# Mamba and mixture-of-experts layer: identity transposes in PE's first gaps, and due times of its own for the second sequence

## The chip, the core and the metric

The kernel runs on one core of a Trainium2 chip. Its engines are TensorE (PE, with its weight loads shown as PEld), VectorE (DVE), ScalarE (ACT), GpSimd (POOL) and SyncE (SP, which only issues transfers here). The metric is the time of one execution on the device, in microseconds (us); lower is better.

## What is computed

The input is 16 sequences of 256 positions with 256 features, all float32. Each sequence is normalised, then goes through two independent layers, and the sum of both and of the input is the output.

```python
xn = _layernorm(x, axis=-1)
x = x + _L0_attn_ref(xn, ...) + _L0_ffn_ref(xn, ...)

# _L0_attn_ref: a state-space (Mamba) layer, 512 channels, 16 states each
proj = jnp.einsum('blh,he->bel', input_states, W_in)
hidden, gate = jnp.split(proj, 2, axis=1)
x = lax.conv_general_dilated(hidden, conv_kernel, ...)[..., :l]      # 4 taps for each channel
hidden = jax.nn.silu(x + conv_bias[None, :, None])
dt, Bm, Cm = jnp.split(ssm_p, [TR, TR + N], axis=-1)                 # ssm_p = hidden x W_x
dts = jax.nn.softplus(jnp.einsum('blr,re->ble', dt, W_dt) + b_dt)
dA = jnp.exp(dts[..., None] * A[None, None])
dBu = dts[..., None] * Bm[:, :, None, :] * hs_ble[..., None]
state = a * state + bu                                               # scan over the positions
y = jnp.einsum('ben,bn->be', state.astype(dtype), c)
y = (scan_out + hidden * D[None, :, None]) * jax.nn.silu(gate)
return jnp.einsum('bel,eh->blh', y, W_out)

# _L0_ffn_ref: 32 experts of width 96, the 8 best of each position, weighted by softmax
rw, sel = jax.lax.top_k(probs, K)
h = jax.nn.silu(x @ wg) * (x @ wu)
acc + h @ wd * w_e[:, None]
```

## The kernel before

All 32 experts are computed densely for every position, and the routing weight (zero for the experts not chosen) scales the hidden values. So for each sequence PE does the same list of products: the turned input (`turn`, L379), the router (`route`, L394), two projections (`project`, `ph`, L517), the step parameters (`params`, `px`, L555, and `widen`, L578), the gate (`pgate`, L697), the output (`po`, L723), and for the experts 24 times a gate product (`pg`), an up product (`pu`, both L471) and a down product (`acc`, L506).

The other engines stand between these. For the Mamba side ACT begins the convolution (L529), DVE adds its other taps (L540), and ACT applies silu (`activate`, `hs`, L547). POOL forms the scan's input (`feed`, `bu`, L630), ACT the decays (`decay`, `da`, L644), DVE runs the scans (L652) and multiplies by C (`read`, `pr`, L664), and an accumulating transfer that POOL issues adds the states up in `y` (L669). For the experts ACT takes the silu of two gate products at once (`silu`, `sg`, L484), POOL multiplies it by the routing weights (`weigh`, L490), which SP has spread over the partitions from memory (`spread`, L457), and DVE multiplies by the up product (`combine`, `h`, L494).

The tiles live in rings of buffers. In PSUM these are g (2 banks), u (2 banks), acc (1 buffer) and da (3 buffers). The gate products and `px` take banks of ring g, the up products banks of ring u.

The order of the work is not written by hand. A planner (class `Plan`, in Python, at build time) holds each step with an engine, a length in us, what it needs, which ring buffers it takes and gives back, and a due time. It plays the program forward, and whenever an engine is free it takes, among the steps that are ready and whose buffers are free, the one with the smallest due time. The order so found is the program; on the chip the waits follow from it, and each engine works in its order. The functions on ACT need tables. A step that names another table than the loaded one costs a table load, and a step whose table is loaded, or that needs none, has `STAY` taken off its due time.

The due time of a step of sequence b is a base time plus offsets by kind:

```python
t = ORIGIN + PERIOD * b
e = ORIGIN + RATE * b + LEAD
due += DUE.get(kind, 0.0) + (FIRST.get(kind, 0.0) if b == 0 else 0.0)
due += LAST.get(kind, 0.0) if b == B - 1 else 0.0
```

The base is `t` for the Mamba side and `e` for the experts. `DUE` holds the offsets of all sequences, `FIRST` and `LAST` are added for the first and for the last one. `EARLY` gives for some kinds how long before its due time a step may start.

At the start PE does 14 transposes of the identity (`warm`, L335 to L338) in a bank of ring g, before any input has come. Then come the router's weights, turned (`turn_router`, L326), and the first x (`turn` of sequence 0). The planner holds `warm` with 6.0 us.

Of the kernel before, what the change touches and what calls it, by code (L numbers as in the profile page):

```python
# [19 lines left out]
class Plan:  # L20
# [7 lines left out]
    SWITCH = 1.3  # L28
    HANDOVER = dict(PE=0.27, DVE=0.14, ACT=0.12, POOL=0.1, SP=0.1)
    MARGIN = dict(PE=0.4, DVE=0.1, ACT=0.1, POOL=0.1, SP=0.0)  # L30
    STAY = 8.6

    def __init__(self, rings):
        self.size = rings
# [86 lines left out]
def mamba_moe_kernel(  # L121
# [30 lines left out]
    nc = tc.nc  # L152
    P = 128
    B, L, H = x.shape
# [7 lines left out]
    SPS = L // P  # L162
# [15 lines left out]
    SLOWEST = 1e-26  # L178
    ORIGIN = -8.4
    PERIOD = 79.3  # L180
    RATE = 79.8

    DUE = dict(
        load_x=-120.5, stats=-16.5, root=-64.0, invert=-262.0, norm=218.5, turn=-490.0,
        keep_turned=-136.0, route=-110.0, largest=-337.5, expo=50.5, choose=-1121.5,
        send_weights=-122.5, project=-72.0, conv_first=402.5, conv_rest=236.0, activate=-361.5,
        params=-140.5, keep_params=-203.5, send_params=-258.5, widen=-105.5, steps=-57.0,
        skip=99.0, inputs=-255.0, fetch=-414.5, feed=399.0, decay=-22.0, scan=427.0, read=68.9,
        collect=-162.5, spread=41.0, gates=-37.5, ups=607.5, silu=230.0, weigh=115.0,
        combine=-69.0, down=114.0, settle=-364.0, gate=38.0, gate_silu=-13.0, fold=508.5,  # L190
        gated=598.5, project_out=-129.5, load_again=-28.5, finish=5.5,
    )
    EARLY = dict(
        load_x=169.0, load_experts=25.0, stats=37.0, turn=155.0, route=255.0, project=501.0,
    )

    FIRST = dict(
        route=248.0, largest=4.5, expo=0.5, choose=551.5, project=287.5, conv_first=-504.5,
        conv_rest=-239.5, activate=150.0, params=-457.5, keep_params=163.5, widen=6.0, steps=770.5,
        skip=-277.5, inputs=137.5, fetch=-152.0, feed=-250.0, decay=-61.0, scan=-50.5, read=-70.5,  # L200
        collect=-120.5, spread=-96.0, gates=-48.0, ups=-216.5, silu=-173.5, weigh=271.5,
        combine=239.0, down=-66.5,
    )

    LAST = dict(
        fetch=-293.5, feed=1.0, decay=252.5, scan=589.0, read=109.5, collect=-95.0, spread=0.5,
        gates=198.5, ups=131.0, silu=192.0, weigh=-110.0, combine=538.5, down=189.5, settle=2.5,
        gate=7.5, gate_silu=223.0, fold=-22.5, gated=238.5, project_out=-415.5, finish=519.5,
    )
    LEAD = -29.6  # L210
    TOPK = 8
    EPS = 1e-5

# [6 lines left out]
    ps = ctx.enter_context(tc.tile_pool(name="ps", bufs=1, space=PSUM))  # L220
# [8 lines left out]
    def take(pool, ring, shape, nm):  # L229
        i = taken[ring] % RINGS[ring]  # L230
        taken[ring] += 1
        return pool.tile(shape, F32, tag=f"{ring}_{i}", name=nm)
# [3 lines left out]
    live = {}  # L236
# [66 lines left out]
    ident = const.tile([P, P], F32, name="ident")  # L303
# [16 lines left out]
    def bank(nm, kind):  # L320
        return take(ps, kind, [P, 512], nm)
# [11 lines left out]


    def warm():  # L335
        pr = bank("warm", "g")
        for i in range(14):
            nc.tensor.transpose(pr[:, :P], ident, ident)  # L338


    def stats(b):
# [405 lines left out]
    b = 0  # L747
# [3 lines left out]
    def add(kind, key, engine, length, due, *args, early=None, **kw):  # L751
        fn = kw.pop("fn", None) or steps_of[kind]
        if early is None:
            early = EARLY.get(kind, 1e9)
        due += DUE.get(kind, 0.0) + (FIRST.get(kind, 0.0) if b == 0 else 0.0)
        due += LAST.get(kind, 0.0) if b == B - 1 else 0.0
        plan.add((kind, *key), engine, length, due, fn, *args, early=early, **kw)

    steps_of = dict(
        load_x=load_x, stats=stats, root=root, invert=invert, norm=norm, turn=turn,  # L760
        keep_turned=keep_turned, route=route, largest=largest, expo=expo, choose=choose,
        project=project, conv_first=conv_first, conv_rest=conv_rest, activate=activate,
        params=params, keep_params=keep_params, widen=widen, steps=steps, skip=skip, inputs=inputs,
        fetch=fetch, spread=spread, gates=gates, ups=expand, silu=silu, combine=combine,
        weigh=weigh, down=down, settle=settle, gate=gate, gate_silu=gate_silu, gated=gated,
        project_out=project_out, load_again=load_again, finish=finish, store=store, feed=feed,
        add_skip=add_skip, fold=fold, send_params=send_params, send_weights=send_weights, collect=collect, decay=decay, scan=scan, read=read,
        turn_router=turn_router, keep_router=keep_router, warm=warm, grow=grow, shrink=shrink, load_router=load_router, load_in=load_in,
        load_steps=load_steps, load_out=load_out, load_experts=load_experts,
    )  # L770
    add("load_router", (), "SP", 0.5, -200.0, lands=3.0)
    add("warm", (), "PE", 6.0, -500.0, takes=[("g", "warm")], gives=["warm"])
    add("turn_router", (), "PE", 0.8, -90.0, needs=[("load_router",)], takes=[("g", "prw")])
    add("keep_router", (), "ACT", 0.3, -89.0, needs=[("turn_router",)], gives=["prw"])
    add("load_in", (0,), "SP", 512 * KB, -199.0, 0, lands=2.0)
# [3 lines left out]
    for j in range(PARTS):  # L779
        for i, kind in enumerate("gud"):  # L780
            due = ORIGIN + LEAD + RATE / PARTS * j + 4.0 * i
# [3 lines left out]
    for b in range(B):  # L785
# [4 lines left out]
            needs=[("turn", b - 1)] if b else [], lands=11.0 if b else 3.5)  # L790
        add("stats", (b,), "DVE", 0.9, t, b, needs=[("load_x", b)],
            takes=[("mv", ("mv", b)), ("st", ("st", b)), ("std", ("rs", b))], gives=[("st", b)])
# [3 lines left out]
            gives=[("mv", b)])  # L796
        add("norm", (b,), "ACT", 1.09, t, b, needs=[("invert", b)],
            gives=[("rs", b)])
        xT = ("xnT", b)
        add("turn", (b,), "PE", 1.0, t, b, needs=[("norm", b)], gives=[x],  # L800
            takes=[("u", ("pt", b)), ("xnT", xT)])
        add("keep_turned", (b,), "ACT", 0.6, t, b, needs=[("turn", b)],
            gives=[("pt", b)])
        add("route", (b,), "PE", 0.9, t if b else t + 30.0, b, needs=[("keep_turned", b), ("keep_router",)],
            takes=[("g", ("pl", b)), ("nmax", ("nmax", b)), ("rest", ("rest", b))], gives=[xT])
# [7 lines left out]
        for q in range(2):  # L813
            add("project", (b, q), "PE", 4 * MM, t, b, q, needs=[("keep_turned", b)] + last + ([("project", b, 0)] if q else []),
                takes=[("gu"[q], ("ph", b, q))] + ([] if q else [("hs", hs)]), gives=[xT])
            add("conv_first", (b, q), "ACT", 0.92, t, b, q, gives=[("ph", b, q)],
                needs=[("project", b, q)] + ([("conv_first", b, 0)] if q else []))
            add("conv_rest", (b, q), "DVE", 2.4, t, b, q,
                needs=[("conv_first", b, q)], gives=[("ph", b, q)])
        add("activate", (b,), "ACT", 1.1, t, b, table="silu",  # L820
            needs=[("conv_rest", b, q) for q in range(2)])
        add("params", (b,), "PE", 8 * MM, t, b, needs=[("activate", b)] + ([] if b else [("load_steps",)]),
            takes=[("g", ("px", b)), ("dt", ("dt", b))])
        add("keep_params", (b,), "ACT", 0.63, t, b, needs=[("params", b)], gives=[("px", b)])
        add("send_params", (b,), "SP", 0.5, t, b, needs=[("keep_params", b)], lands=6.5)
        for q in range(2):
            add("widen", (b, q), "PE", 2 * MM, t, b, q,
                needs=[("keep_params", b)] + ([("widen", b, 0)] if q else []),
                takes=[("gu"[q], ("pdt", b, q))] + ([] if q else [("dts", dts)]),
                gives=[("dt", b)])  # L830
            add("steps", (b, q), "ACT", 0.86, t, b, q, gives=[("pdt", b, q)], table="softplus",
                needs=[("widen", b, q)] + ([("steps", b, 0)] if q else []))
        for c in range(EC):
            u, j = divmod(c, CPU)
            add("skip", (b, c), "ACT", 0.42, t, b, c,
                needs=[("activate", b)] + ([("skip", b, c - 1)] if c else []),
                takes=[] if c else [("sk", ("sk", b))], gives=[hs])
        add("inputs", (b,), "POOL", 2.5, t, b, needs=[("steps", b, 0), ("steps", b, 1),
            ("params", b)] + [("skip", b, c) for c in range(EC)])
        for g in range(GROUPS):  # L840
            at = t + PERIOD / GROUPS * g
            add("fetch", (b, g), "SP", 512 * KB, at, b, g, needs=[("send_params", b)],
                takes=[("rep", ("rep", b, g))], lands=5.5, early=14.0)

        for r in range(UNITS):
            k = UNITS * b + r
            g, u = divmod(r, PAIRED)
            at = t + PERIOD / UNITS * r
            add("feed", (k,), "POOL", 2.31, at, k, needs=[("fetch", b, g), ("inputs", b)],
                takes=[("bu", ("bu", k))], gives=[hs])  # L850
            for j in range(CPU):
# [3 lines left out]
                    takes=[("da", ("da", m))], gives=[dts], table="exp")  # L855
                add("scan", (m,), "DVE", 1.12, when, m, needs=[("decay", m), ("feed", k)],
                    gives=[("bu", k)])
                add("read", (m,), "DVE", 0.6, when, m,
                    needs=[("scan", m)] + ([("read", m - 1)] if j else []),
                    takes=[] if j else [("pr", ("pr", k)) if g else (f"y{u}", ("y", b, u))],  # L860
                    gives=[("da", m), ("rep", b, g)])
            reads = [("read", CPU * k + j) for j in range(CPU)]
            if b == B - 1 and g == GROUPS - 1:
                add("collect", (k,), "DVE", 1.25, at + PERIOD / SLOTS, k, fn=collect_last,
                    needs=reads + [("fold", b, u)], gives=[("pr", k)])
                continue
            if g == 0:
                add("collect", (k,), "POOL", 0.61, at + PERIOD / SLOTS, b, u, fn=add_skip,
                    needs=reads, gives=[("sk", b)], lands=6.5)
                continue  # L870
            add("collect", (k,), "POOL", 0.61, at + PERIOD / SLOTS, k,
                needs=reads + [("collect", k - PAIRED)],
                gives=[("pr", k)], lands=7.8)

        e = ORIGIN + RATE * b + LEAD
        for i in range(PARTS):
            add("spread", (b, i), "SP", 3.0, e + RATE / PARTS * i, b, i,
                needs=[("send_weights", b)], takes=[("wr", ("wr", b, i))], lands=6.0, early=20.0)
        for i in range(PAIRS // BATCH):
            at = e + RATE * BATCH / PAIRS * i  # L880
            qs = range(BATCH * i, BATCH * (i + 1))
            for q in qs:
                part = 2 * q // CPG
                add("ups", (b, q), "PE", 4 * MM, at, b, q, "u", gives=[xT], takes=[("u", ("u", b, q))],
                    needs=[("keep_turned", b)] + ([] if b else [("load_experts", part, "u")]))
                add("weigh", (b, q), "POOL", 1.23, at, b, q, gives=[("wr", b, part)],
                    needs=[("silu", b, i), ("spread", b, part)])
                add("combine", (b, q), "DVE", 0.6, at, b, q,
                    needs=[("weigh", b, q), ("ups", b, q)],
                    takes=[("h", ("h", b, q))], gives=[("u", b, q), ("sg", b, q)])  # L890
                add("down", (b, q), "PE", 4 * MM, at, b, q, gives=[("h", b, q)],
                    needs=[("combine", b, q)] + ([("down", b, q - 1)] if q else [])
                    + ([] if b else [("load_experts", part, "d")]),
                    takes=[] if q else [("acc", ("acc", b))])
            add("gates", (b, i), "PE", 8 * MM, at, b, i, gives=[xT],
                needs=[("keep_turned", b)] + ([] if b else [("load_experts", part, "g")]),
                takes=[("g", ("g", b, q)) for q in qs])
            add("silu", (b, i), "ACT", 1.09, at, b, i, needs=[("gates", b, i)],
                takes=[("sg", ("sg", b, q)) for q in qs], gives=[("g", b, q) for q in qs],
# [3 lines left out]
            gives=[("acc", b)])  # L903

        add("gate", (b,), "PE", 8 * MM, t, b, gives=[xT],
            takes=[(r, (r, "gate", b, q)) for q in range(2) for r in ("g", "gs")],
            needs=[("keep_turned", b)] + ([] if b else [("load_in", 1)]), early=10.0)
        add("gate_silu", (b,), "ACT", 1.09, t, b, needs=[("gate", b)],
            gives=[("g", "gate", b, q) for q in range(2)], table="silu")
# [51 lines left out]
```

## Time and profile before

| what | us |
|---|---|
| median of the runs (lowest to highest, 3 runs) | 1326.89 (1322.99 to 1330.68) |
| the profiled execution, its own time | 1322.61 |
| its span, from the first to the last instruction | 1320.8 |
| mean granted TensorE clock over the span | 0.996 |
| ACT busy in scan decays (`da`, L644) | 468.9 |
| DVE busy in scans (`da`, L652) | 608.2 |
| POOL busy in scan inputs (`bu`, L630) | 715.5 |
| idle time of PE ahead of `pu`, put down to `h` of DVE | 8.6 |

The profile is of one execution. Busy times are those of an engine's instructions. Matmuls overlap, so a busy PE need not be at its peak, and a matmul at half clock counts as busy too. Idle time of an engine is shown ahead of the instruction that ended it, with the instruction that released it behind an arrow. All times on a timeline are counted from the span's start.

### The profile page before, as it was taken

To read this page: it belongs to the slowest core of one execution; us is meant where nothing else is said; L and a number is where in the kernel's file an instruction comes from. 1 tells how busy PE (TensorE), PEld (TensorE's weight loads), DVE (VectorE), ACT (ScalarE), POOL (GpSimd) and SP (SyncE) were. 2 spreads that over 40 slices of the span, in tenths; PEclk is the share of its full clock that TensorE was granted. 3 is DMA by queue.
4 is the path that set the end of the run, shared out by engine and by line. 5 is a ranking of instruction groups with operands and counts; after the bars stand their busy time and mean duration, and the time that the engine had idled before them with its cause. 6 is when DMAs were issued, how large, how long until landed. Compare 5 with 4: busy or idle time off the path is not lost.

```text
span 1320.8 us, 18891 instructions
## 1 busy us (share of the span) xinstructions
PE 1290.6 (98%) x5968; PEld 1108.5 (84%) x5968; DVE 1178.9 (89%) x1735; ACT 1129.6 (86%) x1895; POOL 1184.6 (90%) x803
## 2 busy tenths in 40 slices
PE   8999999999999999999999999999999999999998
PEld 6878888878888887888888888888888888888887
DVE  3688999899989999989999898998989899899986
ACT  5888798888888988899898998989899898988873
POOL 0789899989998998998999999998999989898995
PEclk9999999999999999999999999999999999999999
DMA  9998898898988999999899998999889899998994
GB/s 252 238 254 190 193 212 208 198 210 192 216 187 178 217 219 203 199 197 216 189 216 199 219 204 185 217 198 216 199 194 216 191 205 198 208 205 192 196 222 93
DMA packets 174035, 268.79 MB, mean 204 GB/s; under 512 B 37840, under 2 KB 112112, under 8 KB 173936
## 3 DMA queue, kind: packets, MB, share of 16 engines
q0 software_dynamic: 40672, 124.80, 50.4%
q1 hardware_dynamic: 130624, 142.75, 39.9%
q8 instruction: 47, 0.77, 0.2%
q10 hardware_dynamic: 2640, 0.05, 0.1%
q14 instruction: 52, 0.43, 0.1%
HBM read 137.51 MB, written 5.24 MB: 108 GB/s over the span
## 4 chain that ended last, share of the span: by engine, by line
PE 56%; DVE 13%; POOL 10%; DMA 8%; issue 7%; ACT 5%; SPq 0%; ACTq 0%; POOLq 0%; DVEq 0%
PE pu L471 14%; PE acc L506 14%; PE pg L471 13%; DVE da L652 6%; DMA rep<-bcd 5%; POOL bu L630 4%; PE px L555 4%; DVE pr L664 3%; PE po L723 3%; POOL sg L490 3%; PE ph L517 3%; PE pgate L697 2%; ACT da L644 2%; POOL y L669 2%; PE pdt L578 2%
## 5 line engine op out<-in xcount | busy, mean ns | idle before, releaser
L630 POOL TENSOR_TENSOR bu<-rep,hs 128x1024 f32<-128x1024 f32 x256 | 715.5, 2947 | 68.2 <-DVE da L652 44.2
L652 DVE TENSOR_TENSOR_SCAN da<-da,bu 128x512 f32<-128x512 f32 x512 | 608.2, 1216 | 40.1 <-ACT da L644 36.2
L644 ACT ACTIVATE da<-dts,a_sb 128x256 f32<-128x256 f32 x1024 | 468.9, 473 | 88.2 <-DVE pr L664 64.7
L471 PE MATMUL pu<-xnT,wu_sb 128*128 128x256 f32 x1536 | 361.7, 381 | 9.5 <-DVE h L494 8.6
L506 PE MATMUL acc<-wd_sb,h 128*128 128x256 f32 x1536 | 363.2, 379 | 0.9 <-DVE h L494 0.8
L471 PE MATMUL pg<-xnT,wg_sb 128*128 128x256 f32 x1536 | 349.9, 381 | 4.0 <-ACT sg L484 3.2
L490 POOL TENSOR_TENSOR sg<-sg,wr 128x512 f32<-128x512 f32 x192 | 318.2, 1971 | 34.8 <-ACT sg L484 34.4
L471 PEld LDWEIGHTS pu<-xnT,wu_sb 128*128 128x128 f32 x1536 | 291.3, 191 | 52.3 <-DVE h L494 11.7
L471 PEld LDWEIGHTS pg<-xnT,wg_sb 128*128 128x128 f32 x1536 | 292.4, 191 | 47.0 <-ACT sg L484 5.3
L669 POOL DMA_DIRECT2D y<-pr x222 | 319.8, 1446 | 9.7 <-DVE pr L664 3.7
L506 PEld LDWEIGHTS acc<-wd_sb,h 128*128 128x128 f32 x1536 | 291.2, 190 | 41.3 <-DVE h L494 2.0
L664 DVE TENSOR_TENSOR pr<-da,rep 128x512 f32<-128x512 f32 x448 | 294.2, 677 | 3.4 <-DMA y<-pr 1.6
L644 ACT ACT_TABLE_LOAD x148 | 189.9, 1283 | 2.6
L494 DVE TENSOR_TENSOR h<-pu,sg 128x512 f32<-128x512 f32 x192 | 131.1, 683 | 52.0 <-POOL sg L490 25.3
L484 ACT ACTIVATE sg<-pg 128x512 f32<-128x512 f32 x192 | 105.3, 594 | 8.3 <-PE pg L471 5.5
L484 ACT ACT_TABLE_LOAD x81 | 103.9, 1283 | 3.0 <-PE pg L471 1.6
L540 DVE SCALAR_TENSOR_TENSOR hs<-ph,small,hs 128x255 f32<-128x255 f32 (+2 forms) x192 | 76.1, 471 | 0.0
L713 POOL TENSOR_TENSOR y<-y,gs 128x512 f32<-128x512 f32 x30 | 74.3, 2953 | 0.1
L555 PE MATMUL px<-hs,wx_sb 128*32 128x256 f32 (+1 forms) x256 | 62.8, 393 | 3.0 <-ACT sg L484 3.0
L723 PE MATMUL po<-wout_sb,y 128*128 128x256 f32 x256 | 60.9, 381 | 4.1 <-POOL y L713 3.1
L517 PE MATMUL ph<-xnT,win_sb 128*128 128x256 f32 x256 | 64.3, 397 | 0.0
L688 POOL TENSOR_TENSOR y<-y 128x512 f32<-128x512 f32 x32 | 63.9, 2399 | 0.1
(65 smaller groups left out, 868.5 us busy)
## 6 DMA issues: line engine op xcount, KB each, us to landing
y<-pr POOLq DMA_DIRECT2D x222, 512.0 KB, 7.4
rep<-bcd SPq DMA_DIRECT2D x128, 512.0 KB, 6.1
wr<-wd SPq DMA_DIRECT2D x128, 192.0 KB, 5.4
wr<-wd SPq DMA_DIRECT2D x128, 128.0 KB, 5.5
wr<-wd SPq DMA_DIRECT2D x128, 64.0 KB, 5.3
y<-sk POOLq DMA_DIRECT2D x32, 256.0 KB, 5.9
xt<-L_attn_input_states_dram SPq DMA_DIRECT2D x16, 256.0 KB, 5.7
o<-L_attn_input_states_dram SPq DMA_DIRECT2D x16, 256.0 KB, 6.8
```

Source lines behind the costliest of these rows:

```text
L471: nc.tensor.matmul(p[:, j, :], w[:, hc, ts(c, P)], xs[:, hc, :], start=(hc == 0), stop=(hc == HC - 1),)
L484: nc.scalar.activation(sg, live.pop(("g", b, q)), AF.Silu)
L490: nc.gpsimd.tensor_mul(sg, sg, wr[:, r : r + 2, :])
L494: nc.vector.tensor_mul(h, live.pop(("u", b, q)), live.pop(("sg", b, q)))
L506: nc.tensor.matmul(acc[:, s, :], h[:, j, ts(s, P)], wd_sb[:, c, :], start=(c == 0 and s == 0), stop=(c == FC - 1), skip_group_check=True,)
L517: nc.tensor.matmul(ph[:, j, :], win_sb[:, hc, ts(2 * q + j, P)], xs[:, hc, :], start=(hc == 0), stop=(hc == HC - 1),)
L555: nc.tensor.matmul(p, w[:, c, :], hs[:, c, :], start=(c == 0), stop=(c == EC - 1))
L630: nc.gpsimd.tensor_mul(bu, live["rep", b, g][:, 0:1].to_broadcast([P, CPU, NG, L]), live["hs", b][:, ts(u, CPU), :].unsqueeze(2).to_broadc ...
L644: nc.scalar.activation(da[:, i, :], dts[:, c, :], AF.Exp, scale=a_sb[:, c, n : n + 1])
L652: nc.vector.tensor_tensor_scan(flat, flat, live["bu", k][:, j].rearrange("p n l -> p (n l)"), 0.0, op0=ALU.mult, op1=ALU.add,)
L664: nc.vector.tensor_mul(live["pr", k][:, j], live.pop(("da", m)), live["rep", b, g][:, 1])
L669: nc.gpsimd.dma_start(live["y", b, u].rearrange("p c n l -> p (c n l)"), live.pop(("pr", k)).rearrange("p c n l -> p (c n l)"), accum_op=A ...
```

## The change

`warm` takes its tile from ring acc in place of ring g, and no longer gives it back. A new step `keep_warm` does more transposes of the identity in the same tile: six when the router's weights have been turned, four when the first x has been turned; the second gives the buffer back. The planner's length of `warm` goes from 6.0 to 4.6. A new dict `SECOND` is added to the due times of sequence 1. All other dicts and the constants `STAY`, `RATE` and `LEAD` have new values; `PERIOD` and `ORIGIN` stay. No step of the computation itself is added, removed or cut in another way.

```diff
-    STAY = 8.6
+    STAY = 18.7
...
-    RATE = 79.8
+    RATE = 79.2
...
     DUE = dict(
...
-        load_x=-120.5, stats=-16.5, root=-64.0, invert=-262.0, norm=218.5, turn=-490.0,
+        load_x=-227.0, stats=-16.5, root=60.0, invert=-103.5, norm=315.5, turn=-525.0,
...
-        collect=-162.5, spread=41.0, gates=-37.5, ups=607.5, silu=230.0, weigh=115.0,
+        collect=-168.5, spread=70.0, gates=-34.5, ups=744.0, silu=177.0, weigh=182.5,
...
     EARLY = dict(
-        load_x=169.0, load_experts=25.0, stats=37.0, turn=155.0, route=255.0, project=501.0,
+        load_x=163.0, load_experts=1.0, stats=37.0, turn=13.0, route=225.0, project=631.0,
     )
...
     FIRST = dict(
...
-        collect=-120.5, spread=-96.0, gates=-48.0, ups=-216.5, silu=-173.5, weigh=271.5,
+        read=98.0, collect=-165.0, spread=-304.5, gates=-69.5, ups=-284.5, silu=-159.0,
...
+    SECOND = dict(
+        load_x=-154.5, stats=-69.0, root=-107.0, invert=-72.5, norm=250.5, turn=38.5,
+        keep_turned=-111.0, route=96.0, largest=-100.5, expo=-59.0, choose=13.0,
+        send_weights=-47.5, project=53.0, conv_first=45.5, conv_rest=-55.0, activate=-26.0,
+        params=1.5, keep_params=0.5, send_params=39.5, widen=69.0, steps=36.5, skip=203.5,
+        inputs=-47.0, fetch=-97.5, feed=47.0, decay=-75.5, scan=89.5, read=40.0, collect=-93.5,
+        spread=4.5, gates=-3.5, ups=-204.5, silu=85.5, weigh=-61.0, combine=24.0, down=147.0,
+        settle=-68.5, gate=5.5, gate_silu=-12.5, fold=123.0, gated=-9.5, project_out=-29.5,
+        load_again=-7.0, finish=-55.5,
+    )
...
-    LEAD = -29.6
+    LEAD = -28.8
...
     def warm():
-        pr = bank("warm", "g")
-        for i in range(14):
-            nc.tensor.transpose(pr[:, :P], ident, ident)
+        live["warm"] = take(ps, "acc", [P, SPS, H], "warm")
+        keep_warm(14)
+
+
+    def keep_warm(count):
+        for i in range(count):
+            nc.tensor.transpose(live["warm"][:, 0, :P], ident, ident)
...
         due += DUE.get(kind, 0.0) + (FIRST.get(kind, 0.0) if b == 0 else 0.0)
+        due += SECOND.get(kind, 0.0) if b == 1 else 0.0
...
-    add("warm", (), "PE", 6.0, -500.0, takes=[("g", "warm")], gives=["warm"])
+    add("warm", (), "PE", 4.6, -500.0, takes=[("acc", "warm")])
+    add("keep_warm", (1,), "PE", 1.3, -490.0, 6, needs=[("turn_router",)])
+    add("keep_warm", (2,), "PE", 0.8, -490.0, 4, needs=[("turn", 0)], gives=["warm"])
```

More of the change, by code (lines that the diff above doesn't have):

```diff
@@ L180, in mamba_moe_kernel @@
     PERIOD = 79.3
-    RATE = 79.8
+    RATE = 79.2
     DUE = dict(
-        load_x=-120.5, stats=-16.5, root=-64.0, invert=-262.0, norm=218.5, turn=-490.0,
[L185 to L188, printed above, removed]
-        collect=-162.5, spread=41.0, gates=-37.5, ups=607.5, silu=230.0, weigh=115.0,
-        combine=-69.0, down=114.0, settle=-364.0, gate=38.0, gate_silu=-13.0, fold=508.5,
-        gated=598.5, project_out=-129.5, load_again=-28.5, finish=5.5,
+        load_x=-227.0, stats=-16.5, root=60.0, invert=-103.5, norm=315.5, turn=-525.0,
+        keep_turned=-191.5, route=-108.0, largest=-330.5, expo=181.0, choose=-1176.5,
+        send_weights=-270.5, project=-11.0, conv_first=565.0, conv_rest=249.0, activate=-364.0,
+        params=-161.0, keep_params=-256.5, send_params=-231.5, widen=-198.5, steps=-84.5,
+        skip=155.0, inputs=-291.5, fetch=-267.5, feed=336.0, decay=-39.0, scan=499.0, read=54.9,
+        collect=-168.5, spread=70.0, gates=-34.5, ups=744.0, silu=177.0, weigh=182.5,
+        combine=-139.0, down=231.0, settle=-483.5, gate=33.0, gate_silu=21.5, fold=501.0,
+        gated=721.0, project_out=-35.0, load_again=-24.0, finish=41.5,
@@ L192, in mamba_moe_kernel @@
     )
     EARLY = dict(
-        load_x=169.0, load_experts=25.0, stats=37.0, turn=155.0, route=255.0, project=501.0,
+        load_x=163.0, load_experts=1.0, stats=37.0, turn=13.0, route=225.0, project=631.0,
     )
     FIRST = dict(
-        route=248.0, largest=4.5, expo=0.5, choose=551.5, project=287.5, conv_first=-504.5,
-        conv_rest=-239.5, activate=150.0, params=-457.5, keep_params=163.5, widen=6.0, steps=770.5,
-        skip=-277.5, inputs=137.5, fetch=-152.0, feed=-250.0, decay=-61.0, scan=-50.5, read=-70.5,
@@ L201, in mamba_moe_kernel @@
-        collect=-120.5, spread=-96.0, gates=-48.0, ups=-216.5, silu=-173.5, weigh=271.5,
-        combine=239.0, down=-66.5,
+        route=226.0, largest=50.5, expo=-140.0, choose=605.0, project=291.0, conv_first=-613.0,
+        conv_rest=-473.0, activate=178.5, params=-415.0, keep_params=180.0, widen=-45.5,
+        steps=918.5, skip=-362.5, inputs=212.0, fetch=-196.0, feed=-325.5, decay=-113.5, scan=-2.5,
+        read=98.0, collect=-165.0, spread=-304.5, gates=-69.5, ups=-284.5, silu=-159.0,
@@ new lines, in mamba_moe_kernel @@
+        weigh=204.0, combine=285.0, down=32.0,
+    )
[8 more added lines that the diff above has]
+        load_again=-7.0, finish=-55.5,
@@ L203, in mamba_moe_kernel @@
     )
     LAST = dict(
-        fetch=-293.5, feed=1.0, decay=252.5, scan=589.0, read=109.5, collect=-95.0, spread=0.5,
-        gates=198.5, ups=131.0, silu=192.0, weigh=-110.0, combine=538.5, down=189.5, settle=2.5,
-        gate=7.5, gate_silu=223.0, fold=-22.5, gated=238.5, project_out=-415.5, finish=519.5,
+        fetch=-110.5, feed=8.5, decay=300.5, scan=555.0, read=-52.0, collect=-306.5, spread=-123.0,
+        gates=198.5, ups=84.0, silu=464.5, weigh=-183.0, combine=520.0, down=355.0, settle=-92.0,
@@ L209, in mamba_moe_kernel @@
+        gate=-58.0, gate_silu=123.0, fold=-114.5, gated=367.0, project_out=-485.5, finish=535.0,
     )
-    LEAD = -29.6
+    LEAD = -28.8
     TOPK = 8
@@ L767, in mamba_moe_kernel @@
         add_skip=add_skip, fold=fold, send_params=send_params, send_weights=send_weights, collect=collect, decay=decay, scan=scan, read=read,
-        turn_router=turn_router, keep_router=keep_router, warm=warm, grow=grow, shrink=shrink, load_router=load_router, load_in=load_in,
+        turn_router=turn_router, keep_router=keep_router, warm=warm, keep_warm=keep_warm, grow=grow, shrink=shrink, load_router=load_router, load_in=load_in,
         load_steps=load_steps, load_out=load_out, load_experts=load_experts,
```

## The prediction

> **What bounds the kernel now.** I read the page's busy shares first. Five engines are all above 85%, and a 98% for PE says little, because it is a mean over stages.
>
> ```profile
> PE 1290.6 (98%) x5968; PEld 1108.5 (84%) x5968; DVE 1178.9 (89%) x1735; ACT 1129.6 (86%) x1895; POOL 1184.6 (90%) x803
> ```
>
> So I cut the span into stages and asked for the busy time of each engine in each (columns: stage, its length, busy time of PE, PEld, DVE, ACT, POOL with counts, granted TensorE clock, DMA share, GB/s).
>
> ```profile
> 8.47:31.78 23.31, 20.30 (x73) 15.75 (x74) 9.52 (x33) 12.81 (x21) 2.50 (x2) 0.93 0.96 281
> 31.78:78.00 46.22, 45.60 (x217) 38.84 (x216) 31.72 (x54) 39.69 (x65) 35.13 (x23) 1.00 0.93 242
> 78.00:120.00 42.00, 37.40 (x156) 31.37 (x155) 37.10 (x50) 34.41 (x60) 36.29 (x24) 0.92 0.97 222
> 120.00:660.00 540.00, 527.85 (x2455) 452.13 (x2454) 500.95 (x730) 469.45 (x797) 502.58 (x337) 1.00 0.90 202
> 660.00:1160.00 500.00, 499.97 (x2345) 433.94 (x2344) 460.13 (x680) 451.03 (x751) 467.04 (x317) 1.00 0.93 205
> 1160.00:1316.90 156.90, 154.48 (x712) 132.65 (x710) 137.50 (x185) 118.75 (x200) 140.29 (x96) 1.00 0.84 183
> ```
>
> Length minus PE busy is PE's idle time: 3.01, 0.62, 4.60, 12.15, 0.03 and 2.42 us. From 660 to 1160 PE never stops: the matrix products are the bound, and no new order can gain there. After 1316.9 only a sum and the store remain (3.9 us). What can be won lies in the idle time, and in stretches where PE runs slowly while it counts as busy. For these I read PE's own timeline at the start (start, length, instruction, count, idle time before it).
>
> ```profile
> 1.37 3.25 PE L338 MATMUL warm<-ident 128*128 128x128 f32 x14 [1.37 <-POOL eps_sb L306]
> 4.55 0.42 PE L326 MATMUL prw<-ident,rw_sb 32*128 32x32 f32 x2
> 6.40 1.40 PE L379 MATMUL pt<-ident,xt 128*128 128x128 f32 x4 [1.44 <-ACT xt L370]
> 8.47 1.91 PE L394 MATMUL pl<-rwT,xnT 128*128 128x32 f32 x8 [0.68 <-ACT xnT L384]
> 10.20 6.44 PE L517 MATMUL ph<-xnT,win_sb 128*128 128x256 f32 x16
> 16.47 3.62 PE L471 MATMUL pg<-xnT,wg_sb 128*128 128x256 f32 x16
> 19.93 3.62 PE L471 MATMUL pu<-xnT,wu_sb 128*128 128x256 f32 x16
> 26.55 5.23 PE L555 MATMUL px<-hs,wx_sb 128*32 128x256 f32 x16 [3.01 <-ACT sg L484]
> ```
>
> Two groups stand out. The 16 products `ph` take 6.44 us, and the 16 of the same shape right after them 3.62. The 16 `px` take 5.23 us, but 3.77 in the chain that ended last at 234.03. Both are half-clock work. For `px` the clock column says so (0.50 from 26 to 29). For `ph` it shows 1.00; there the durations are the evidence, the column is not. ACT's timeline tells why PE was idle ahead of `px`:
>
> ```profile
> 21.53 1.06 ACT L547 ACTIVATE hs<-hs 128x1024 f32<-128x1024 f32 x1
> 22.60 1.28 ACT L353 ACT_TABLE_LOAD   x1
> 23.90 0.30 ACT L353 ACTIVATE rstd<-mv,eps_sb 128x2 f32<-128x2 f32 x1
> ...
> 24.61 1.28 ACT L484 ACT_TABLE_LOAD   x1
> 25.90 1.09 ACT L484 ACTIVATE sg<-pg 128x512 f32<-128x512 f32 x2
> ```
>
> Between two uses of the silu table ACT goes to sqrt and back for the root of the second sequence. `px` needs a bank of ring g, and both hold `pg` until `sg` has read them.
>
> **The change, part by part.** The sum is made against the profiled execution: 1322.61 us, span 1320.8. It is at the fast end of the runs shown; the median 1326.89 lies 4.28 above it, which I add at the end.
>
> *The identity in the gaps.* Six transposes go behind the router's, four behind the first x. At the 231 ns between such transposes in the `warm` row they need 1.39 and 0.92 us; the idle times there are 1.44 and 0.68. The first six fit. The four would delay the router's products by 0.24 us if the clock is still low, and fit at 141 ns each (the weight load of later transposes): 0 to +0.25, I take 0. The `warm` tile moves from ring g to ring acc, whose first product starts at 35.51, so nobody waits for it.
>
> *What an open clock gives.* `ph` 6.44 - 3.62 = 2.8 us; the router's 8 products at 231 - 141 ns for each load, 0.7. Together 3.5, all of it on PE's path. In the trace the first burst is busy from 1.37 to 4.97 = 3.6 us, and yet the work behind it stayed slow up to about 15.8. The Trainium skill ("TensorE: Matmul & The Clock Gate", Part 1: The HAM clock gate) says that one busy window of about 3.4 us opens the clock, that the windows run free of the kernel's start, and that the ramp is best not fitted. By that rule 3.6 us of transposes can be enough already, the addition gains nothing in such a run, and my sum is smaller by 3.5. By the row they were not enough: a window must fall wholly inside, and only a longer burst ensures that. With the gaps filled, PE is busy from 1.37 to 8.5, which holds a whole window wherever it begins. Bounds 0 (a transposed identity doesn't count, or this run's window was unlucky in before and others were not) to 3.5; I take the row, 3.5.
>
> *The order on ACT.* A step's due time is its stage's plus the dicts' offsets, less STAY if its table is loaded. Before, when `activate` of sequence 0 ends: silu(0,0) is -38.0 + 230 - 173.5 = 18.5, less 8.6 = 9.9; root(1) is 70.9 - 64 = 6.9. Root wins. After: silu(0,0) is -37.2 + 177 - 159 - 18.7 = -37.9; root(1) is 70.9 + 60 - 107 = 23.9. Silu wins by far. So `sg` follows `hs` directly, 25.90 - 22.60 = 3.3 us sooner, one table load (1.28) is saved, and PE's 3.01 us wait goes. With it the clock doesn't drop, and `px` needs 3.77 instead of 5.23: 1.46 more. 4.47 together. What is late next: `hs` itself, behind DVE's convolution. That starts at 15.30, after `ph`; with faster `ph` it is held by the routing steps on DVE (11.27 to 13.18, 0.7 earlier), so it starts near 12.5, and `hs` and `sg` end near 19.8 and 20.9. PE gets to `px` at 23.55 - 3.5 = 20.0: 0.9 of wait is left. Net of both: -3.5 - 4.5 + 0.9 = -7.1 us.
>
> Does it pass on? The first `h` waits for POOL, and POOL needs the weights' rows, which SP starts to spread at 19.66 behind the routing. This moves by 0.7 at most. In after, `px` ends at 20.9 + 3.8 = 24.7, one more batch of `pg` fills PE to 28.2, and the first `h` is there at 28.6 even unmoved. So 0.4 is lost: -6.7.
>
> *Due times of the second sequence.* Two waits carry this stage, with the slow clock behind them:
>
> ```profile
> 97.74 3.63 PE L471 MATMUL pu<-xnT,wu_sb 128*128 128x256 f32 x8 [2.54 <-DVE h L494]
> ...
> 113.61 5.41 PE L471 MATMUL pg<-xnT,wg_sb 128*128 128x256 f32 x16 [1.89 <-ACT sg L484]
> ```
>
> Idle 4.4; slow work 3.63 - 1.89 (8 products elsewhere) and 5.41 - 3.62, 3.5: 7.9 in all. The new offsets act on just these steps, but which wait goes can't be read from a trace of before. Bounds: -7.9, and +2.5 (one more wait like the longer). I take half the gain, -4.0: the two waits have different causes, and one removed brings its clock with it.
>
> *STAY, RATE and the other offsets.* A longer STAY saves table loads (308 at 1283 ns, 395 us of ACT). The dense stage hides them all: there they are worth 0. In 120:660 and the last stage the 14.6 us of idle may go or grow. From -14.6 to +20 (below); I take 0, as no row favours a side.
>
> Sum: -6.7 - 4.0 = -10.7; 1322.61 - 10.7 = 1311.9; plus 4.28, 1316.2: **1316 us**, 0.8% faster. About 0.5% (1320.3 to 1333.5) is what a measurement of this kernel can tell from no change.
>
> **Rivals.** *The later stalls go too:* the other half of the second sequence and half of 14.6: -11.3 more, 1305. For it: the idle of 120:660 is a handful of waits (2.54 for POOL's `y` at 228, 2.24 for `h` at 282), not steady. Against: DVE and POOL are 93% busy there, with little room to catch up.
>
> *The clock isn't opened:* identity transposes may not count, and the first 3.25 us of them opened nothing. Then 3.5 is missing: 1319.5.
>
> *The head start is swallowed:* the scan work on DVE and POOL (93%) sets when PE gets its `y` and `h`, and what PE gains early it waits for before 660. About 3 us survive: 1324, no change. For it: 12.15 us of PE idle follow the ramp now.
>
> *Slower: STAY turns into a wait in every sequence.* ACT holds exp up to 18.7 us past a silu's due time; ring g has two banks, one batch of `pg` fills both, and PE, in order, stops behind it. Now this wait costs PE 3.2 us in all. If it comes once a sequence, at the 2.4 us of the stalls seen, in 14 sequences: 33.6 - 14.6 there now = +19, with the -10.7: 1335. It decides from (14.6 + 10.7) / 14 = 1.8 us a sequence. Against it: in the dense stage PE has about 0.03 us of idle, so buffers now cover the switches; ACT is 90% busy there.
>
> **How the numbers follow.** Forecast 0.34, later stalls too 0.20, clock not opened 0.12, swallowed 0.18, slower 0.16. Faster by over 0.5%: the first two and two thirds of the third, 0.62; within: 0.22; slower: 0.16. The range goes from 1303, just under the better case, to 1332, which cuts most of the slower one.
>
> **What would show it.** Right: `ph` x16 in about 3.6 us; `sg` right behind `hs` on ACT with no sqrt load between; `px` in 3.8 us, ending near 25; less than 1.2 us of PE idle before it; 78:120 with under 3 us of PE idle and a clock above 0.95. Wrong: `ph` still over 6 us; a `pg` or `pu` wait of 2 us that returns every 79 us beyond 660; or the head 7 us early and 120:660 with some 20 us of idle.

## The result: slower by 0.9%, and the profile after

The changed kernel takes 1337.47 us (median of 6 runs, 1331.53 to 1340.64) beside 1324.76 for the kernel before. The ratio is 1.009, with a 95% interval from 1.0068 to 1.0113. The profiled execution has a span of 1336.0 us, 15.2 more than before. Lines moved by 11 to 15: `nmr`, L361 before, is L376 now, `h` L509, `bu` L645.

First the busy shares on the page, then the same stages as in the prediction (length, busy time of PE, PEld, DVE, ACT, POOL with counts, granted clock, DMA share, GB/s).

```profile
PE 1295.0 (97%) x5978; PEld 1111.4 (83%) x5978; DVE 1185.3 (89%) x1735; ACT 1132.6 (85%) x1897; POOL 1184.1 (89%) x803
```

```profile
8.47:31.78 23.31, 23.16 (x101) 19.14 (x100) 9.42 (x33) 15.44 (x28) 4.33 (x4) 1.00 0.95 268
31.78:78.00 46.22, 45.16 (x211) 38.12 (x209) 33.99 (x57) 40.06 (x67) 31.69 (x20) 1.00 1.00 246
78.00:120.00 42.00, 33.83 (x145) 28.48 (x146) 35.91 (x47) 32.11 (x52) 38.47 (x26) 0.96 0.91 206
120.00:660.00 540.00, 517.20 (x2382) 441.33 (x2380) 491.97 (x718) 460.23 (x777) 490.66 (x332) 0.99 0.90 197
660.00:1160.00 500.00, 498.69 (x2332) 432.19 (x2333) 459.68 (x674) 449.56 (x748) 465.21 (x314) 1.00 0.93 204
```

PE's idle time is 0.15, 1.06, 8.17, 22.80 and 1.31 us; before it was 3.01, 0.62, 4.60, 12.15 and 0.03. The first stage lost its wait, as forecast. The two behind it gave 4.0 us back, and 120 to 660 lost another 10.7. The busy shares on the page hardly show this: PE goes from 98 to 97%, the others move by at most a point.

What PE waits for shows it better (in all, times, longest). First a row of before, then the same row of the changed kernel:

```profile
PE acc L506 <- DVE h L494: 0.8, 1, 0.8
```

```profile
PE acc L521 <- DVE h L509: 20.8, 14, 4.1
```

In the new order the experts' down product comes to PE before its `h` is there, 14 times in place of once.

The head, on PE's timeline and on ACT's:

```profile
10.26 5.53 PE L532 MATMUL ph<-xnT,win_sb 128*128 128x256 f32 x16
...
22.84 3.84 PE L570 MATMUL px<-hs,wx_sb 128*32 128x256 f32 x16
```

```profile
21.24 1.06 ACT L562 ACTIVATE hs<-hs 128x1024 f32<-128x1024 f32 x1
22.20 1.06 ACT L499 ACTIVATE sg<-pg 128x512 f32<-128x512 f32 x2
```

`sg` follows `hs` with no table load between, `px` starts without a wait and at full clock, and it ends at 26.68 in place of 31.78: 5.1 us ahead. `ph` still takes 5.53 us, so in this execution PE came to full clock only inside it.

Where do the 22.8 us come from? The first long stall of PE is `acc` at 191.38, which waits 4.12 us for `h`. In DVE's queue this `h` stands behind one small instruction (the products `pr` between them are left out):

```profile
185.27 4.26 DVE L376 SCALAR_TENSOR_TENSOR nmr<-mv,rstd 128x2 f32<-128x2 f32 x1
...
190.65 0.67 DVE L509 TENSOR_TENSOR h<-pu,sg 128x512 f32<-128x512 f32 x1
```

What `nmr` waits for is seen most clearly at 361: two of DVE's lines, then two of POOL's for the same time.

```profile
360.54 0.15 DVE L373 RECIPROCAL rstd<-rstd 128x2 f32<-128x2 f32 x1
360.72 4.31 DVE L376 SCALAR_TENSOR_TENSOR nmr<-mv,rstd 128x2 f32<-128x2 f32 x1
```

```profile
360.70 3.09 POOL L645 TENSOR_TENSOR bu<-rep,hs 128x1024 f32<-128x1024 f32 x1
363.01 2.00 POOL L505 TENSOR_TENSOR sg<-sg,wr 128x512 f32<-128x512 f32 x1
```

`nmr` works on two elements a partition and takes 0.16 us when POOL has no product under way. Here it takes 4.31 and ends at 365.03, when POOL's second product ends (363.01 + 2.00 = 365.01). (POOL's records overlap a little, and its spans are rough.) In the traces of both kernels each `nmr` of over 1 us, 20 in all, ends 15 to 29 ns after the end of a product of POOL, and up to three such products end while it waits. DVE works in order, so what stands behind `nmr` waits as well: at 185 the products `pr`, ACT's next `da` (4.02 us for `pr`) and `h`, and then PE. The view of one tile's instructions shows the same wait in the kernel before (least, median and longest duration in ns):

```profile
L361 DVE SCALAR_TENSOR_TENSOR nmr<-mv,rstd x16: 160/282/4740, 5.6 to 1147.2; 128x2 f32<-128x2 f32 x16
```

It had three long ones, of 4.3 to 4.7 us, at 270, 352 and 516; the changed kernel has four of 3.3 to 4.3, at 185, 273, 361 and 528. Their lengths are alike; what PE loses behind them is larger in the changed kernel. It also depends on the place: behind the 4.26 us at 185 PE waits 4.12 us, behind the 4.31 at 361 only 0.88 (at 367).

```profile
191.38 3.68 PE L521 MATMUL acc<-wd_sb,h 128*128 128x256 f32 x8 [4.12 <-DVE h L509]
...
277.16 3.48 PE L521 MATMUL acc<-wd_sb,h 128*128 128x256 f32 x8 [2.80 <-DVE h L509]
...
532.80 3.66 PE L521 MATMUL acc<-wd_sb,h 128*128 128x256 f32 x8 [2.86 <-DVE h L509]
```

Eight such products take 1.89 us at full clock. With each of these three stalls they take 3.5 to 3.7, so the clock had dropped (granted 0.64 in 192 to 196, 0.72 in 278 to 282 and in 534 to 538). The stalls of before behind its own long `nmr` (2.24 us at 282, 2.25 at 529) were shorter, and the clock stayed at 1.00.

### The profile page after: what moved, and what is told of

Read it like the earlier page. It is cut to its first block, busy times and chain, and to the rows that moved or that the text cites. A ratio compares the mean times of both kernels' runs of the same rounds, so it can differ in the third digit from the quotient of the medians.

```text
span 1336.0 us, 18926 instructions
## 1 busy us (share of the span) xinstructions
PE 1295.0 (97%) x5978; PEld 1111.4 (83%) x5978; DVE 1185.3 (89%) x1735; ACT 1132.6 (85%) x1897; POOL 1184.1 (89%) x803
## 4 chain that ended last, share of the span: by engine, by line
PE 60%; DVE 10%; POOL 10%; DMA 7%; ACT 6%; issue 6%; SPq 1%; DVEq 0%; POOLq 0%; ACTq 0%
PE acc L521 15%; PE pu L486 15%; PE pg L486 15%; DVE da L667 4%; POOL bu L645 4%; PE ph L532 3%; PE po L738 3%; PE px L570 3%; PE pgate L712 3%; ACT da L659 3%; DVE pr L679 3%; POOL sg L505 2%; DMA rep<-bcd 2%; DMA wr<-wd 2%; POOL y L684 2%
## 5 line engine op out<-in xcount | busy, mean ns | idle before, releaser
L645 POOL TENSOR_TENSOR bu<-rep,hs 128x1024 f32<-128x1024 f32 x256 | 727.2, 2967 | 72.8 <-DVE da L667 39.0
L521 PE MATMUL acc<-wd_sb,h 128*128 128x256 f32 x1536 | 369.8, 384 | 20.8 <-DVE h L509 20.8
L505 POOL TENSOR_TENSOR sg<-sg,wr 128x512 f32<-128x512 f32 x192 | 321.6, 1993 | 29.0 <-DMA wr<-wd 25.4
L684 POOL DMA_DIRECT2D y<-pr x222 | 313.4, 1418 | 28.1 <-DVE pr L679 10.6
L509 DVE TENSOR_TENSOR h<-pu,sg 128x512 f32<-128x512 f32 x192 | 130.8, 682 | 65.1 <-POOL sg L505 44.2
L703 POOL TENSOR_TENSOR y<-y 128x512 f32<-128x512 f32 x32 | 69.6, 2591 | 0.4 <-DMA y<-pr 0.4
L728 POOL TENSOR_TENSOR y<-y,gs 128x512 f32<-128x512 f32 x30 | 67.7, 2592 | 0.2
```

The costliest lines, as they stand in the source:

```text
L505: nc.gpsimd.tensor_mul(sg, sg, wr[:, r : r + 2, :])
L509: nc.vector.tensor_mul(h, live.pop(("u", b, q)), live.pop(("sg", b, q)))
L521: nc.tensor.matmul(acc[:, s, :], h[:, j, ts(s, P)], wd_sb[:, c, :], start=(c == 0 and s == 0), stop=(c == FC - 1), skip_group_check=True,)
L645: nc.gpsimd.tensor_mul(bu, live["rep", b, g][:, 0:1].to_broadcast([P, CPU, NG, L]), live["hs", b][:, ts(u, CPU), :].unsqueeze(2).to_broadc ...
L684: nc.gpsimd.dma_start(live["y", b, u].rearrange("p c n l -> p (c n l)"), live.pop(("pr", k)).rearrange("p c n l -> p (c n l)"), accum_op=A ...
```

## The experiments

My theory from these lines: the new order puts `nmr` beside POOL's products at places where PE has little in hand, and this makes the loss. Rivals: the ten transposes, the longer STAY, the due times of the second sequence, late transfers.

**The transposes alone.** `a_nowarm` is the changed kernel without them, `b_warm` is the kernel before with them; the order of all else is kept.

```diff
 def keep_warm(count):
-    for i in range(count):
+    for i in range(count if count > 6 else 0):
```

> The changed kernel without its ten extra transposes; every other instruction stays in its place. If the new order of the work makes the loss, the time stays near 1337 us (1331 to 1341) and ph x16 takes 5 to 6.5 us, as with the transposes, which then do nothing for the clock. If the transposes open the clock early in some executions, the time rises by about 3 us. If the transposes themselves cost, it falls toward 1325.

> The kernel before with the same ten transposes in the same two gaps, its order of work kept. If identity transposes don't count for the clock: ph x16 in 5 to 6.5 us and a time within 3 us of before (about 1325). If they do: ph x16 in 3.6 us and about 1321.

`a_nowarm` took 1336.12 us, ratio to before 1.0083 (1.0063 to 1.0103); `b_warm` 1324.1, ratio 0.9992 (0.9976 to 1.0007). So the transposes neither make the loss nor bring a measurable gain. Neither case that I expected of `b_warm` came about: `ph` is fast in its profile, and the time is that of before.

```profile
L523 PE MATMUL ph<-xnT,win_sb x16: 379/379/462, 9.1 to 12.5; 128*128 128x256 f32 x16
```

The median product takes 379 ns, against 600 ns in `a_nowarm`'s. Over the profiles of all 14 kernels, `ph` x16 took 3.7 us in 8 of the 11 executions with the ten transposes and 5.1 us or more in the 3 without. That looks like their work, but in most cases it isn't. Here are the first six of the ten in two executions, `a_nosecond_nmr` and the changed kernel:

```profile
4.84 0.88 PE L353 MATMUL warm<-ident 128*128 128x128 f32 x6
```

```profile
4.89 1.54 PE L353 MATMUL warm<-ident 128*128 128x128 f32 x6
```

In 5 of the 8 the six took 0.88 to 0.96 us, so the clock was open when they had hardly begun: what PE does ahead of them in both kernels was enough there, and in other executions it was not. In the other three (`a_nmr_half`, `a_stay`, `b_warm`) the six took 1.37 to 1.54 and the clock opened about at their end; only there can they have opened it. Whether they kept it open in the five is not shown. And in 3 of the 11, the changed kernel's among them, all ten changed nothing: `ph` took 5.3 to 5.6 us.

**`nmr` without its second tensor.** `a_nmr` and `b_nmr` are the two kernels with `nmr` computed by two instructions that take 1/std as a scalar operand.

```diff
-nc.vector.scalar_tensor_tensor(
-    nmr, mv[:, :, 0:1], -1.0, rstd, op0=ALU.mult, op1=ALU.mult
-)
+for s in range(SPS):
+    nc.vector.tensor_scalar(
+        nmr[:, s, :], mv[:, s, 0:1], rstd[:, s, :], -1.0, ALU.mult, ALU.mult
+    )
```

> The changed kernel with nmr, two elements a partition, made by two instructions that take 1/std as a scalar operand in place of one that reads two tensors in SBUF. If nmr, which took up to 4.3 us of DVE beside POOL's products, starts most of PE's stalls from 120 on: nmr under 0.4 us, PE idle in 120 to 660 from 22.8 to below 12 us, time 1325 to 1329. If late rep transfers and the experts' order do it: idle above 18 us, time 1333 or more.

> The kernel before with the same other form of nmr. If nmr starts most of the stalls from 120 on: PE idle in 120 to 660 from 12.2 to below 6 us, time 1317 to 1320. If not: idle above 10 us, time 1323 to 1327.

`a_nmr` took 1317.5 us, ratio 0.9945 (0.9925 to 0.9965), and `b_nmr` 1315.8, ratio 0.993 (0.9907 to 0.9953). The changed kernel gains 20.0 us against its 1337.5, more than expected; the kernel before gains 8.5 against the 1324.35 measured beside it. What is left between the two is 1.7 us, within their intervals (each ratio is known to about 3 us). DVE, ACT and POOL carry out the same instructions in the same order in both forms, `nmr` apart. So about 11 of the 12.7 us between before and after come through this one instruction, under the new order. In `a_nmr`'s profile, the tile's line, the ramp, and the stage of the first stall:

```profile
L377 DVE TENSOR_SCALAR nmr<-mv,rstd x32: 203/210/215, 5.7 to 1142.1; 128x1 f32<-128x1 f32 x32
```

```profile
120.00:660.00 540.00, 528.82 (x2464) 453.66 (x2463) 490.69 (x739) 475.20 (x803) 504.56 (x341) 1.00 0.92 204
...
180.00:200.00 20.00, 20.00 (x96) 17.62 (x95) 19.18 (x28) 19.49 (x33) 20.00 (x14) 1.00 0.90 184
```

PE's idle time in 120 to 660 goes from 22.8 to 11.2 us; in `b_nmr` it goes from 12.15 to 6.75, where I had expected less than 6. `acc` still waits 9.5 us for `h` in `a_nmr`, against 2.4 in `b_nmr`: this part belongs to the order. The three drops of the clock of the changed kernel (each 3.5 to 3.7 us of products that take 1.9) cost some 5 more, and none is left after 120 in `a_nmr`. So the profiles show where the changed kernel gains: 11.6 us of idle and 5 of slow work in this stage. They don't add up to the 11, which is the difference of two gains. The profile of `b_nmr` is of the slowest of its six runs (1320.02 us), and its clock drops twice after 120, at 232 and 392, where before has no drop.

**Is it the second tensor?** `a_nmr_tt` splits `nmr` in a plain product of the same two tensors and a change of sign.

```diff
+nc.vector.tensor_mul(nmr, mv[:, :, 0:1], rstd)
+nc.vector.tensor_scalar(nmr, nmr, -1.0, None, ALU.mult)
```

> The changed kernel with nmr as a plain product of the two tensors in SBUF, then a change of sign by a second instruction with one tensor. If it is the second tensor operand in SBUF that waits for POOL: the product takes up to 4 us, the change of sign 0.2 us, time 1333 or more. If it is the form with a scalar and two tensors alone: both short, time 1316 to 1322.

1335.5 us, ratio 1.0088 (1.0071 to 1.0106). The tile's lines:

```profile
L376 DVE TENSOR_TENSOR nmr<-mv,rstd x16: 160/1318/4303, 5.4 to 1162.8; 128x2 f32<-128x2 f32 x16
L377 DVE TENSOR_SCALAR nmr<-nmr x16: 169/170/195, 5.6 to 1164.1; 128x2 f32<-128x2 f32 x16
```

The product of two tensors in SBUF waits as before, the instruction with one tensor never does. The Trainium skill says this ("SBUF — State Buffer", Who interferes with whom): a DVE instruction with two SBUF inputs shares a read port with a GpSimd instruction that reads SBUF, as an exclusive lock, and the one that comes second blocks until the first has finished. The traces agree that it blocks. They differ on how long: at 361 `nmr` started at 360.72, ahead of POOL's second product (363.01), and still waited until that one had ended, and elsewhere for three in a row. That the cause is the port is the page's account; the runs show that it is the second tensor in SBUF beside POOL's products.

**Where it costs.** `a_nmr_half` keeps the two-tensor form for the first eight sequences and takes the scalar form after.

```diff
+if b < 8:
     nc.vector.scalar_tensor_tensor(...)
+else:
+    for s in range(SPS): nc.vector.tensor_scalar(...)
```

> The changed kernel; nmr reads two tensors in SBUF for the first eight sequences only and takes a scalar operand for the others. If the long waits of the ramp (3.3 to 4.3 us at 185, 273, 361 and 528) cost the time: as slow as the changed kernel, 1333 to 1339. If the waits of 1.1 to 1.6 us in every later sequence cost it: 1317 to 1324.

1332.74 us, ratio 1.0063 (1.0042 to 1.0083). That is just below the 1333 to 1339 expected of the ramp and far from 1317 to 1324. So most of the cost of `nmr`, 15 of 20 us, is paid in the first eight sequences. The medians leave about 4.7 us for the later waits of 1.1 to 1.6 us, but there the intervals of the two ratios overlap.

**The parts of the new due times.** `a_stay` puts STAY back to 8.6, `a_nosecond` leaves SECOND out; both keep the two-tensor `nmr`. `a_nosecond_nmr` is `a_nosecond` with the scalar form.

```diff
-    STAY = 18.7
+    STAY = 8.6
...
-        due += SECOND.get(kind, 0.0) if b == 1 else 0.0
+        due += 0.0
```

> The changed kernel with STAY back at 8.6, all else as changed, nmr with two tensors. If the longer stay at a table costs PE a wait in every sequence: the time falls to about 1327. If the order's nmr waits make it: the time goes with the sum of nmr before 660, over 18 gives 1333 or more, under 15 gives 1328 or less.

> The changed kernel without the due times of the second sequence, all else as changed, nmr with two tensors. If the loss is a matter of where nmr falls beside POOL's products, the time goes with the sum of nmr before 660 (15.3 us in before, 18.8 in the changed kernel): over 18 gives 1333 or more, under 15 gives 1328 or less. If the second sequence's due times themselves cost: 1325 to 1330 with the sum of nmr unchanged.

> The kernel without the second sequence's due times, now with the scalar form of nmr. Its order is the one with the longest nmr of all (6.5 us in every second sequence after 660, 47 us in all) and with 18.4 us of PE idle in the dense stage. If nmr's waits make that idle time: below 3 us of PE idle in 660 to 1160 and a time of 1325 to 1340. If the order itself is short of buffers there: idle stays above 12 us, 1355 or more.

`a_stay` took 1339.05 us, ratio 1.0101 (1.0071 to 1.0132), so STAY put back doesn't help. It doesn't clear STAY either, because it makes another order on DVE, ACT and POOL: PE's idle time in 120 to 660 falls to 11.9 us, and a new wait comes near the end:

```profile
1325.47 6.38 PE L738 MATMUL po<-wout_sb,y 128*128 128x256 f32 x16 [8.61 <-DVE y L699]
```

What STAY alone is worth stays open, as with RATE, LEAD and the other dicts, which were not put back one by one. `a_nosecond` took 1368.5, ratio 1.0332 (1.0306 to 1.0358): beside these other due times, the offsets of the second sequence save time and don't cost it. `a_nosecond_nmr` took 1344.46, ratio 1.0162 (1.0121 to 1.0203).

The sums of `nmr` in these expectations were wrong. Added up from the trace's instructions, `nmr` takes 17.7 us before 660 in the kernel before and 18.6 in the changed one; and the sum told nothing: `a_stay` has 15.9 and `a_nosecond` 16.8, and neither is faster than the changed kernel. What an `nmr` costs depends on where it falls, as at 185 and 361. In `a_nosecond` it falls on three products of POOL in every second sequence of the dense stage, 6.5 us each time. First `a_nosecond`'s dense stage, then that of `a_nosecond_nmr`:

```profile
660.00:1160.00 500.00, 481.56 (x2229) 412.63 (x2228) 454.51 (x649) 425.74 (x710) 444.16 (x301) 1.00 0.89 193
```

```profile
660.00:1160.00 500.00, 489.64 (x2283) 421.68 (x2282) 443.37 (x669) 436.80 (x729) 453.47 (x307) 1.00 0.91 198
```

The scalar form takes PE's idle from 18.4 to 10.4 us, between the two theories: `nmr` makes under half of it, the order the rest.

**Where the head start goes.** With the scalar form the head of `a_nmr` is still 5.5 us ahead of `b_nmr` (`px` starts at 20.8 against 26.3), and yet it ends no sooner. POOL waits 6.89 us for a `rep` transfer at 71 and 2.13 at 79. `a_nmr_fetch` issues this `rep` ahead of the last up weights; `a_nmr_loads` moves three weight transfers forward.

```diff
+moved = steps.pop(name.index(("fetch", 0, 3)))                       # a_nmr_fetch
+steps.insert(name.index(("load_experts", 3, "u")), moved)
...
+move(("load_experts", 2, "u"), ("load_x", 2))                        # a_nmr_loads
+move(("load_experts", 2, "d"), ("send_weights", 1))
+move(("load_in", 1), ("send_weights", 1))
```

> The changed kernel with the scalar form of nmr, and one rep transfer of the first sequence (the fourth) issued by SP ahead of the last up weights in place of behind them. If the head start is lost because this rep comes late behind weights: POOL's wait of 6.9 us at 71 falls below 3.5, PE idle in 78 to 120 from 6.0 to below 4, time 1 to 4 us under 1317.5. If DVE and POOL set the pace anyway: POOL waits less there and elsewhere more, time within 1.5 us of 1317.5.

> The changed kernel with the scalar form of nmr, and three weight transfers of SP moved ahead, into a stretch in which SP waits and the DMA engines are at 128 GB/s (45 to 50): the third part of the up weights, the third of the down weights, the gate half of the input projection. If the head start is lost to weights and rep transfers that share 55 to 80: POOL's rep waits of 6.9 and 2.1 us before 82 fall below 4 together, PE idle in 78 to 120 from 6.0 to below 4, time 2 to 4 us under 1317.5. If DVE and POOL set the pace: the idle time comes back before 660, time within 1.5 us.

`a_nmr_fetch` took 1320.42 us, ratio 0.9972 (0.9961 to 0.9983), `a_nmr_loads` 1319.29, ratio 0.9953 (0.9938 to 0.9969). Neither is faster than `a_nmr`; both lie 1.8 to 2.9 us above it, a little outside what either case allowed. In `a_nmr_fetch` POOL no longer waits at 71; it waits at 81, for the next `rep`:

```profile
81.23 2.33 POOL L651 TENSOR_TENSOR bu<-rep,hs 128x1024 f32<-128x1024 f32 x1 [10.88 <-DMA rep<-bcd]
```

In `a_nmr_loads` POOL waits 1.73 us at 69 and 7.94 at 82, and PE's idle time in 78 to 120 is 8.3 us, not below 4. So the theory of one late transfer, or of these weights in its way, falls: the wait moves and is as long in sum (10.9 and 9.7 against 9.0). What sets the pace of `rep` in this stage, its ring of three buffers, SP's order or the load on the DMA engines, stays open.

**The best of what was seen.** `b_nmr_warm` is the kernel before with the scalar form and the transposes.

> The kernel before with the scalar form of nmr and the ten transposes in the gaps: the best of what was seen. If an open clock at the start is worth something here: 1312 to 1314. If the start is swallowed later: within 1.5 us of 1315.8.

1314.39 us, ratio 0.9924 (0.9908 to 0.994): 0.8% faster than before, and not to be told from `b_nmr`.

## Why the prediction was wrong, point by point

- *What an open clock gives (-3.5).* I took the row of one execution against the rule quoted beside it. In 5 of the profiles it is as the rule has it: what stands ahead of the added transposes was enough, and they come too late to open anything. My own step, that PE busy from 1.37 to 8.5 opens the clock wherever a window begins, failed in 3 of 11. Worth at the end: nothing measurable (`b_warm` 0.9992).
- *The order on ACT (-4.5).* Right: no sqrt load between `hs` and `sg`, `px` in 3.84 us without a wait, 5.1 us ahead at its end (7.1 forecast, with the clock).
- *"Does it pass on?" (-6.7).* Wrong. I followed it only to the first `h`. The head start was lost before 120: idle of 31.78 to 120 went from 5.2 to 9.2 us, while POOL's waits for `rep` in 60 to 120 went from 4.7 to 9.5. This was my rival "swallowed", sooner than it said. With the scalar form in both kernels nothing is left of the 10.7 us that I forecast: 1317.5 against 1315.8.
- *Due times of the second sequence (-4.0).* Wrong: idle of 78 to 120 rose from 4.60 to 8.17, though the clock there went from 0.92 to 0.96, as forecast.
- *"STAY, RATE and the other offsets" (0).* This is the step that failed most. I took 0 because no row favoured a side, and gave the range no reason beyond STAY. The 12.15 us of idle were called "a handful of waits", and I didn't follow one of them back. The `nmr` row of before (160/282/4740 ns) would have led to a small DVE instruction that waits on POOL's products, and whose place a new order shuffles. In place of 0, this stage took 10.7 us more of idle and some 5 of slow clock in the profile; by the medians, about 11 us of the loss come through `nmr`.
- *The rival on the slower side* had about the right time (1335) and the wrong mechanism: `pg` waits for `sg` 4.5 us in all (3.2 before), in four waits and not in every sequence, and STAY put back doesn't help. That its time was near is luck.
- *The signs.* "The head 7 us early and 120:660 with some 20 us of idle" came about nearly as written (5.1 and 22.8 us), but not by the path that I gave it: half of that idle goes with the form of `nmr`.
- The range ended at 1332 because I gave that rival 0.16 and cut it; the time was 5 us outside. One reading was off without bearing on the sum: of the five shares called above 85%, PEld's is 84.

## What to carry to other kernels

Before a change of order, look for instructions of one form whose longest duration is many times their shortest: they may wait for something that the order decides. Here the form of one such instruction, of 0.16 us and at times blocked for 4, was worth 8.5 us in the kernel before, where the whole change gained nothing. A DVE instruction with two tensors in SBUF shouldn't stand in the queue beside long POOL products when a form with a scalar operand does the same. And a head start in one engine counts only as far as the transfers behind it can follow: trace it to the first stage where another engine has its input late.

## What was not expected of the hardware

A DVE instruction that waits for POOL is not let in when the product under way ends, if the next one has started by then: it waited through up to three in a row, 4.7 us in the kernel before and 6.6 in `a_nosecond`. Each of the changed kernel's three long stalls of PE (2.8 to 4.1 us) cost another 1.6 to 1.8 us by the drop of the clock. But the length of a stall does not decide alone whether the clock drops. The same wait of nearly the same length, first in before, then in `b_nmr`:

```profile
228.59 1.99 PE L723 MATMUL po<-wout_sb,y 128*128 128x256 f32 x8 [2.54 <-POOL y L713]
```

```profile
231.62 3.68 PE L724 MATMUL po<-wout_sb,y 128*128 128x256 f32 x8 [2.59 <-POOL y L714]
```

The eight products take 1.99 us in one and 3.68 in the other. What else decides it, these runs don't show.
